# A gated cross-attention and mixture-of-experts layer: the opening by pairs of tiles with two sum-free products first, smaller key stores, and the last routing step's rows at the far end of each expert's slots

## The chip, the cores and the metric

The kernel runs on one core of one Trainium2 chip. The metric is the device time of one execution in microseconds (us), of which several runs are taken; one further execution is profiled.

## The reference, cut to what matters

All data is float32. x is 4096 rows of 512, ctx is 3202 rows of 512.

```python
def attn(hc, hq):            # hc = layernorm(x), hq = ctx
    Sim = (hc @ w1)[:, None] + (hq @ w2)[None, :] + (hc * w3) @ hq.T + b_sim
    hq_hat = softmax(Sim, axis=1) @ hq
    hc_bar = softmax(Sim.max(axis=1)) @ hc
    feats  = concat([hc, hq_hat, hc * hq_hat, hc * hc_bar])
    return feats @ W_qv + b_qv

def moe(xf):                 # xf = layernorm(x), E = 8 experts, top 2, cap = 640 slots each
    gates = softmax(xf @ w_router + b_router)
    topv, topi = top_k(gates, 2)
    pos  = running count of earlier choices of the same expert
    keep = pos < cap
    buf[e, pos] = xf[token] where kept
    out  = gelu(buf @ w1 + b1) @ w2 + b2      # 512 -> 2048 -> 512 per expert
    y    = sum over the two choices of gate * out, divided by the sum of the kept gates
    return y

x = x + tanh(g_xattn) * attn(layernorm(x), ctx)
x = x + tanh(g_ffn)   * moe(layernorm(x))
```

Which slot of its expert a kept token gets does not matter, as long as no two tokens share one and the token is found again.

## The kernel before, in words

Nearly all matrix products are done as seven block products instead of eight (the Winograd form of Strassen's scheme): with a left matrix in blocks A11 to A22 and a right one in blocks B11 to B22, sums S1, S2, S4 (and A11 − A21) of the left and T1, T2, T4 (and B22 − B12) of the right are made on VectorE first. The products are named "1" (A11·B11), "2" (A12·B21), "6", "7", "5", "4", "3"; only "1" and "2" use raw blocks of both sides. Results are put together from the products by additions (u2, u3) on VectorE as they come.

The attention works on eight groups of 512 rows of x (a group is four tiles of 128 rows). For each group, stage S multiplies the scaled queries `Qp` with the key tiles: 12 tiles `kt` of 2 × 128 context rows in six pairs, one call of `chain` for each pair (product at L512), followed by 128 left-over rows. In group 0 (`stage_a_first`, `build`) the key tiles come raw from `ctxt_t`, a transposed copy of the context made on the host. VectorE adds the four sums (L364 to L368), and ScalarE's queue stores the whole tile of seven blocks to `kt_d`; later groups load these seven blocks with one transfer (`load_keys`). The stages D, E and V, with softmax and values, follow; they are not touched.

The opening comes before the first pair: `stage_a_first` loads four tiles of x on SyncE, and `layernorm` makes each one's statistics (L93, L95), its factor on GpSimd (L99, L100) and its normalised form (L102). TensorE transposes it (L110), ScalarE copies it to `qT`, and pieces `Qp` are made of two tiles at a time (L212, L214). `right_sums` makes the T blocks.

Each engine's instructions stand in one order, and an instruction that waits holds up all behind it on its engine. `tc.issue_after(i)` keeps an instruction behind another in that order. DMAs are issued from an engine's queue in the same order; SyncE's carries nearly all loads. SBUF tiles come from pools: `st` has five buffers for key tiles, so a sixth tile's load waits until the first one's tile has been read by TensorE and stored.

After the eight groups come the routing steps, in which 32 tiles are taken in steps of 4 (six times) and 2 (four times). For each step TensorE makes `x1p` (L1062), `choose` finds the two experts of each row on VectorE, and `place` counts the slots (`pos`, L1167 and L1168) and writes the slot numbers `sidx`. `dispatch` scatters each tile's rows to `buf_d` in DRAM with one indirect DMA per choice (L1198, on GpSimd's queue; 64 in all). The steps are overlapped: a step's rows are placed and sent while the next is computed. Behind the last step there is nothing to overlap with; `idle_work` gives TensorE 7 and then 11 matmuls of no use (`idle`, L1218).

The experts come last. `expert_in` loads five tiles `xb` of 128 rows from an expert's 640 slots (L1335), transposes them (L110) and makes the T blocks. For each half of the hidden layer there are four calls of `seven` (f = 0 to 3, 28 products of 128×320, L1299), with Gelu on ScalarE (L1421), then the output products (`op`, L1462). For expert 0 each of the five loads is made to wait for every scatter:

```python
if e == 0:
    for i in scatters:
        tc.add_manual_dep(ld.ins, i.name, ..., reason="every token is in its slot")
```

The scatters are declared free of dependences among themselves, because their slots are distinct.

Of the kernel before, what the change touches and what calls it, by code (L numbers as in the profile page):

```python
# [20 lines left out]
def gated_layer(ctx, tc, x, x_t, ctxt, ctxt_t, ctxt_c, ctxt_r, g_xattn, g_ffn, w_sim, w_sim_r, b_sim, W_qv, W_qv_t, b_qv, b_qv_c, w_router, b_router, w1, b1, w2, b2, out):  # L21
# [35 lines left out]
    nc.scalar.dma_start(ws, w_sim)  # L57
# [4 lines left out]
    nc.scalar.dma_start(bsim, b_sim.partition_broadcast(P))  # L62
    gx = const.tile([P, 1], F32, name="gx")
    nc.scalar.dma_start(gx, g_xattn.partition_broadcast(P))
    gf = const.tile([P, 1], F32, name="gf")
    nc.scalar.dma_start(gf, g_ffn.partition_broadcast(P))
    bqv = const.tile([P, D], F32, name="bqv")
    tgx, tgf = gx, gf
    nc.scalar.activation(tgx, gx, AF.Tanh)
    nc.scalar.activation(tgf, gf, AF.Tanh)  # L70
# [13 lines left out]
    nc.scalar.dma_start(wrc, w_router.rearrange("(c p) e -> p c e", p=P))  # L84
    we = const.tile([P, 4, DC, E], F32, name="we")
    sd = const.tile([P, NT], F32, name="sd")

    scales, normed = [], []

    def layernorm(sm, dst, src, t):  # L90
        st = sm.tile([P, 6], F32, name=f"st{t}", tag="st")
        with tc.issue_after(normed[-2]) if len(normed) > 1 else ExitStack():
            nc.vector.bn_stats(st, src)  # L93
        mv = sm.tile([P, 2], F32, name=f"mv{t}", tag="mv")
        nc.vector.bn_aggr(mv, st)  # L95
        rstd = sm.tile([P, 1], F32, name=f"rstd{t}", tag="rstd")
        ve = sm.tile([P, 1], F32, name=f"ve{t}", tag="ve")
        with tc.issue_after(scales[-1]) if scales else ExitStack():
            nc.gpsimd.tensor_scalar(ve, mv[:, 1:2], EPS, None, ALU.add)  # L99
        scales.append(nc.gpsimd.tensor_tensor(rstd, ve, neghalf, ALU.pow).ins)  # L100
        nc.gpsimd.tensor_tensor(sd[:, t : t + 1], ve, rstd, ALU.mult)
        nrm = nc.vector.tensor_scalar(dst, src, mv[:, 0:1], rstd, ALU.subtract, ALU.mult)  # L102
        normed.append(nrm.ins)
        return nrm

    def transposed(pool, src, name):

        ps = pool.tile([P, DC, P], F32, name=name, tag="tr")
        for c in range(DC):
            nc.tensor.transpose(ps[:, c, :], src[:, c * P : (c + 1) * P], ident)  # L110
        return ps

# [11 lines left out]
    with ExitStack() as s1:  # L124
# [10 lines left out]
        kt_d = [dram.tile([P, 7, 2, P], F32, name=f"kt_d{j}", tag=f"kt_d{j}") for j in range(NJ)]  # L135

        kc_d = dram.tile([P, 4, 2, P], F32, name="kc_d", tag="kc_d")
        KSLOT = {"1": 0, "2": 1, "7": 2, "4": 3, "5": 4, "6": 5, "3": 6}
# [8 lines left out]
        nc.scalar.dma_start(bcol, b_qv_c)  # L147
# [17 lines left out]
        nc.scalar.dma_start(cr, ctxt_r)  # L165
# [19 lines left out]
        def right_sums(g, qT, Qp):  # L185

            B11, B12, B21, B22 = (Qp[:, r : r + 2, c : c + 256] for r in (0, 2) for c in (0, 256))
            T1, T2, T4 = (sb.tile([P, 2, 256], F32, name=f"q{k}_{g}", tag=f"qt{k}") for k in (1, 2, 4))
            tt(T1, B12, B11, ALU.subtract)
            t2 = tt(T2, B22, T1, ALU.subtract)  # L190
            tt(B12, B22, B12, ALU.subtract)
            tt(T4, B21, T2, ALU.subtract)
            live[g] = {"qT": qT, "t2": t2, "B": {"1": B11, "6": T2, "7": B12, "5": T1, "2": B21, "4": T4, "3": B22}}

        def stage_a_first():

            qT = sb.tile([P, DC, TG], F32, name="qT0", tag="qT", bufs=2)
            Qp = sb.tile([P, DC, TG], F32, name="Qp0", tag="Qp")
            qs = []
            for t in range(4):  # L200
                q = sb.tile([P, D], F32, name=f"q{t}", tag="q" if t < 3 else "mb", bufs=3 if t < 3 else 1)
                nc.sync.dma_start(q, x[t * P : (t + 1) * P, :])
                layernorm(sm, q, q, t)
                ps = transposed(ps_tr, q, f"qps{t}")
                cp = nc.scalar.copy(qT[:, :, t * P : (t + 1) * P], ps)
                qs.append(q)
                if t % 2:
                    h = slice((t - 1) * P, (t + 1) * P)
                    for c in range(DC):
                        w3, w2 = ws[:, 2 * DC + c : 2 * DC + c + 1], ws[:, DC + c : DC + c + 1]  # L210
                        if c < DC // 2:
                            qp = ts(Qp[:, c, h], qT[:, c, h], w3, w2, ALU.mult, ALU.add)  # L212
                        else:
                            live["qp"] = nc.scalar.activation(Qp[:, c, h], qT[:, c, h], AF.Identity, scale=w3, bias=w2)  # L214
                    if t == 1:
                        live["norm"] = qp
                if t == 2:
                    with tc.issue_after(cp.ins):
                        nc.scalar.dma_start(wv[:, 0, :], w_sim_r[:D].partition_broadcast(P))
                        nc.scalar.dma_start(  # L220
                            wv[:, 1:, :].rearrange("p r d -> p (r d)"), ctxt[L - NR :, :].flatten().partition_broadcast(P)
                        )
                        nc.scalar.dma_start(bqv, b_qv.partition_broadcast(P))
            right_sums(0, qT, Qp)
            nc.scalar.dma_start(qT_d[0], qT)
            return qs
# [10 lines left out]
        def stage_a_rest(qs):  # L237
# [13 lines left out]
            ps = ps_tr.tile([P, DC, P], F32, name="wrps", tag="tr")[:, 0, :E]  # L251
            for c in range(DC):
                nc.tensor.matmul(ps, ones, wrc[:, c, :], start=c == 0, stop=c == DC - 1)
            mean = be
            ts(mean, ps, 1.0 / D, None, ALU.mult)
            tt(wrc, wrc, mean.unsqueeze(1).to_broadcast([P, DC, E]), ALU.subtract)
# [100 lines left out]

        def build(j):

            kt = st.tile([P, 7, 2, P], F32, name=f"ktb{j}", tag="st")  # L360
            queue.append(nc.sync.dma_start(kt[:, 0:4].rearrange("p a b w -> p (a b) w"), ctxt_t[:, j, :, :]))
            A11, A12, A21, A22, S1, S2, S4 = (kt[:, k, :, :] for k in range(7))
            with tc.issue_after(live["norm"].ins if j < 2 else live[0]["t2"].ins):
                tt(S1, A21, A22, ALU.add)  # L364
                tt(S2, S1, A11, ALU.subtract)
            with tc.issue_after(live[0]["t2"].ins):
                tt(S4, A12, S2, ALU.subtract)
                tt(A21, A11, A21, ALU.subtract)  # L368
            return kt
# [60 lines left out]
        def load_keys(g, j):  # L430
            kt = st.tile([P, 7, 2, P], F32, name=f"kt{g}_{j}", tag="st")
            queue.append(nc.sync.dma_start(kt, kt_d[j]))
# [26 lines left out]
        def chain(name, prod, done):  # L459
# [5 lines left out]
            prod(pa, "1", True, False)  # L465
# [6 lines left out]
            tt(u2, p6, p1, ALU.add)  # L472
# [7 lines left out]
            prod(pa, "2", False, True)  # L480
            nc.scalar.copy(done(0, 0), pa)  # L481
# [6 lines left out]
        def stage_s(g):  # L488
# [4 lines left out]
            kts = {}  # L493
            if g == 0:
                for j in PAIRS[0]:
                    kts[j] = build(j)
            for jj, js in enumerate(PAIRS):
                if g == 0:
                    for j in PAIRS[jj + 1] if jj + 1 < len(PAIRS) else []:
                        kts[j] = build(j)  # L500
# [16 lines left out]
                e_add = chain(f"s{g}_{jj}", prod, lambda i, j: e[:, j, i, :, :])  # L517
                if g == 0:
                    for j in js:
                        nc.scalar.dma_start(kt_d[j], kts[j])  # L520
# [454 lines left out]
    with ExitStack() as s2:  # L975
# [49 lines left out]
        scatters = []  # L1025


        STEPS = [list(range(t, t + G)) for t in range(0, NT - 2 * G, G)]
        STEPS += [list(range(t, t + G // 2)) for t in range(NT - 2 * G, NT, G // 2)]
# [18 lines left out]
        def tile_mm(s, i):  # L1048
# [11 lines left out]
            for j in range(2):  # L1060
# [5 lines left out]
            stt(  # L1066
                x1.rearrange("p (j d) -> p j d", j=2), ps[:, :, :256], tgx, r[:, :, :256], ALU.mult, ALU.add,
                accum_out=s.sum[:, i : i + 1],
            )
# [23 lines left out]
        def choose(s):  # L1093
# [56 lines left out]
            for i in range(n):  # L1150
# [6 lines left out]
                tt(dst, s.base[:, i, :], s.mask[:, i, :], ALU.add)  # L1157

        def place(s):
# [16 lines left out]
            ts(keep, keep, float((E + 1) * CAP), None, ALU.is_lt)  # L1176

# [16 lines left out]
            if s.next is not None and s.next.n == 2:  # L1194
                placed.append(done.ins)

        def dispatch(s, i, k):
# [8 lines left out]
            scatters.append(sc.ins)  # L1206

            tc.declare_no_dep(scatters[-1], group="scatters", reason="slots are unique")
            tc.add_to_no_dep_group("scatters", scatters[-1])
# [3 lines left out]
        placed = []  # L1213
        def idle_work(mm, n):

            for _ in range(n):
                with tc.issue_after(mm.ins):
                    mm = nc.tensor.matmul(idle, ones, wv[:, 0, :], start=True, stop=True)  # L1218
# [3 lines left out]
        prev, s = None, begin(0)  # L1222
# [3 lines left out]
        def send(n):  # L1226
            for _ in range(min(n, len(routed))):
                dispatch(*routed.pop(0))
# [6 lines left out]
        for g in range(len(STEPS)):  # L1235
# [5 lines left out]
            if s.n > 2:  # L1241
                with tc.issue_after(mm.ins):
                    place_prev()
                send(4)
                for i in range(2, s.n):
                    tile_mm(s, i)
            sc = scale(s)
            if s.n == 2:
                with tc.issue_after(mm.ins):
                    place_prev()  # L1250
            with tc.issue_after(sc.ins):
                send(4 if s.n > 2 else 5)
# [4 lines left out]
        idle_work(prev.counted, 11)  # L1257
# [8 lines left out]
    with ExitStack() as s3:  # L1266
# [28 lines left out]
        def seven(tag, n, A11, A12, A22, S1, S2, S3, S4, B11, B21, B22, T1, T2, T3, T4, done):  # L1295

            def prod(ps, A, B, start=True, stop=True):
                for i, (a, b) in enumerate(zip(A, B)):
                    nc.tensor.matmul(  # L1299
# [254 lines left out]
```

## Time and profile before

| | us |
|---|---|
| median of 4 runs | 2638.25 (2637.54 to 2639.9) |
| profiled execution, its own time | 2638.75 |
| its span, first to last instruction | 2636.7 |
| TensorE busy | 2606.5 |
| VectorE busy | 1703.2 |
| ScalarE busy | 461.5 |
| GpSimd busy | 237.3 |
| first attention product starts | 12.91 |
| routing steps end, hand-over begins | about 1607 |
| first product of expert 0 starts | 1631.67 |
| output products of expert 0 start | 1664.01 |

Starts are counted from the first instruction. A matmul line of the profile groups several records; a product of stage S is eight records (two tiles × two blocks, two records for each matmul), and a product of an expert is four. The mean granted clock of TensorE over the span is 0.995.

### The profile page before, as it was taken

How to read it: one execution, taken by the hardware profiler on the slowest of the kernel's cores; microseconds unless marked ns; L12 is line 12 of the kernel's file. 1: busy time of each engine (PE TensorE's matmuls, PEld its weight loads, DVE VectorE, ACT ScalarE, POOL GpSimd, SP SyncE). 2: the span in 40 equal slices, each digit the busy share in tenths (PEclk: the TensorE clock that was granted, in tenths of full speed). 3: DMA queues.
4: the chain of work that ended last, by engine and by line, in shares of the span. 5: the costliest groups of instructions: out<-in, count | busy, mean ns of one | idle time of the engine just before them, and what ended most of it. 6: DMA issues, size and time to landing. Idle time of an engine off the chain costs nothing. (4 is left out here: it accounts for less than half of the span.)

```text
span 2636.7 us, 29718 instructions
## 1 busy us (share of the span) xinstructions
PE 2606.5 (99%) x11236; PEld 2103.1 (80%) x11236; DVE 1703.2 (65%) x3412; ACT 461.5 (18%) x796; POOL 237.3 (9%) x288
## 2 busy tenths in 40 slices
PE   8999999999999999999999999999999999999998
PEld 7748888888888888888888886777777777777776
DVE  7858856947668569478475567464756565565654
ACT  1201201201102002012020143112121111111111
POOL 0111000000001000000000055010101010101010
PEclk9999999999999999999999999999999999999999
DMA  8497656746746657467446795131324132322210
GB/s 314 152 284 243 212 175 190 246 147 180 255 159 195 220 160 241 161 186 248 154 140 207 265 356 185 65 124 64 128 78 144 67 128 89 104 92 100 76 60 21
DMA packets 182959, 436.07 MB, mean 165 GB/s; under 512 B 17454, under 2 KB 84270, under 8 KB 180768
## 3 DMA queue, kind: packets, MB, share of 16 engines
q1 hardware_dynamic: 150208, 352.25, 40.6%
q0 software_dynamic: 16096, 45.04, 5.0%
q10 hardware_dynamic: 16512, 36.88, 3.9%
q8 instruction: 89, 1.46, 0.2%
q14 instruction: 54, 0.44, 0.1%
HBM read 355.71 MB, written 85.55 MB: 167 GB/s over the span
## 5 line engine op out<-in xcount | busy, mean ns | idle before, releaser
L512 PE MATMUL pas<-Qp,kt 128*128 128x256 f32 x672 | 160.5, 380 | 0.0
L1299 PE MATMUL pah<-bT,w 128*128 128x320 f32 x512 | 159.8, 434 | 0.5 <-ACT p1h L1306 0.5
L662 PE MATMUL pbv<-E,vt 128*128 128x256 f32 x672 | 147.3, 379 | 0.0
L662 PEld LDWEIGHTS pbv<-E,vt 128*128 128x128 f32 x672 | 127.7, 190 | 17.3
L512 PEld LDWEIGHTS pas<-Qp,kt 128*128 128x128 f32 x672 | 127.2, 190 | 17.4 <-issue 0.5
L1299 PEld LDWEIGHTS pah<-bT,w 128*128 128x128 f32 x512 | 97.3, 190 | 39.7 <-ACT p1h L1306 1.0
L603 ACT ACTIVATE E<-E 128x1024 f32<-128x1024 f32 x96 | 100.9, 1057 | 129.5 <-DVE E L602 128.7
L602 DVE TENSOR_TENSOR E<-E,mb 128x1024 f32<-128x1024 f32 x96 | 116.0, 1224 | 11.4 <-ACT mb L589 11.4
L1299 PE MATMUL pao<-w,h 128*128 128x256 f32 x512 | 120.9, 379 | 0.0
L1485 POOL DMA_INDIRECT out<-acc,ti x40 | 41.0, 1024 | 852.8 <-DVE acc L1484 843.1
L1062 PE MATMUL x1p<-W,q2T 128*128 128x264 f32 x512 | 116.1, 387 | 0.0
L1462 PE MATMUL op<-w,h 128*128 128x512 f32 x256 | 114.8, 593 | 0.0
L1299 PEld LDWEIGHTS pao<-w,h 128*128 128x128 f32 x512 | 97.3, 190 | 20.0 <-issue 7.7
L1062 PEld LDWEIGHTS x1p<-W,q2T 128*128 128x128 f32 x512 | 96.7, 190 | 16.1
L468 ACT COPY p1s<-pas 128x512 f32<-128x512 f32 x48 | 28.2, 586 | 437.4 <-issue 257.1
L538 DVE TENSOR_TENSOR M<-M,E 128x1024 f32<-128x1024 f32 x80 | 98.0, 1225 | 4.3
L693 PE MATMUL vv<-E,vc 128*128 128x512 f32 x192 | 94.3, 622 | 0.5 <-ACT E L603 0.5
L1462 PEld LDWEIGHTS op<-w,h 128*128 128x128 f32 x256 | 46.6, 190 | 48.7 <-issue 43.0
L1423 DVE TENSOR_TENSOR h<-p4h,u3h 128x320 f32<-128x320 f32 x64 | 31.3, 490 | 78.0 <-PE p4h L1299 78.0
L481 ACT COPY E<-pas 128x512 f32<-128x512 f32 x48 | 28.1, 585 | 303.8 <-PE pas L512 286.7
L611 DVE TENSOR_TENSOR SM<-SM,E 128x1024 f32<-128x1024 f32 x64 | 78.6, 1227 | 2.5 <-ACT E L603 2.5
L484 DVE TENSOR_TENSOR E<-p4s,u3s 128x512 f32<-128x512 f32 x48 | 33.1, 689 | 72.2 <-PE p4s L512 72.2
(449 smaller groups left out, 5467.8 us busy)
## 6 DMA issues: line engine op xcount, KB each, us to landing
kt<-kt_d SPq DMA_DIRECT2D x84, 896.0 KB, 4.7
w<-in_w SPq DMA_DIRECT2D x32, 2048.0 KB, 9.2
vt<-vs_d SPq DMA_DIRECT2D x56, 768.0 KB, 7.1
wp<-wt_d SPq DMA_DIRECT2D x56, 520.0 KB, 4.6
kt_d<-ktb ACTq DMA_DIRECT2D x12, 896.0 KB, 4.6
buf_d<-zero SPq DMA_DIRECT2D x80, 129.0 KB, 5.9
xb<-buf_d SPq DMA_DIRECT2D x40, 258.0 KB, 4.0
r<-r_d SPq DMA_DIRECT2D x32, 260.0 KB, 6.2
```

Of the source, the lines that this page charges most:

```text
L484: tt(done(1, 0), p4, u3, ALU.add)
L512: nc.tensor.matmul(ps[:, jl, :], kts[j][:, KSLOT[p], k, :], B[p][:, k, :], start=start and jl == 0 and k == 0, stop=stop and k == 1, skip_ ...
L538: tt(M, M, e[:, :, h], ALU.max)
L602: live[g]["last"] = tt(e, e, m, ALU.subtract)
L603: live[g]["exp"] = nc.scalar.activation(e, e, AF.Exp)
L611: tt(SM, E_t[0][:, lr] if jj == 1 else SM, E_t[jj][:, lr], ALU.add)
L662: nc.tensor.matmul(ps[b], vt[:, j - i * JH, b * P : (b + 1) * P], right(j) if j < NJ else right_c, start=start and j == 0 and b == 0, stop ...
L693: mm = nc.tensor.matmul(ps[b], vc[:, h, b * P : (b + 1) * P], E[j // 2][:, :, h, j % 2, :] if j < NJ else ec, start=j == 0 and h == 0, sto ...
L1062: mm = nc.tensor.matmul(ps[:, j, :B1], qTs[g][:, c, q * P : (q + 1) * P], W1[:, c, j, :], start=(c == 0), stop=(c == DC - 1))
L1299: nc.tensor.matmul(ps, a, b, start=start and i == 0, stop=stop and i == len(A) - 1, skip_group_check=True)
L1462: nc.tensor.matmul(ps, hT[:, k, 2 * MH :], W2[:, k, :], start=(k == 0), stop=(k == KH - 1))
L1485: sc = nc.gpsimd.indirect_dma_start(out=out[:, :], out_offset=rows_of(ti, s), in_=acc[:, :], in_offset=None, bounds_check=N - 1, oob_is_er ...
```

## The change

Four things are changed.

1. *Opening.* The constants' loads are issued on ScalarE after a Tanh of one column that needs no load, and five matmuls of no use (`warm`) and the router-mean matmuls come first on TensorE. The four x loads are issued back to back, then the raw key tiles of pair 0. Statistics and factors are made for two tiles at a time, then the four normalisations, in a written-out order. The context's transposed copy has its second half rolled so that the raw blocks come as A11, A12, A22, A21. In the first pair `chain` runs the products "1" and "2" first, into separate banks, and adds their results on VectorE; the key sums are interleaved with the query pieces and the right sums.
2. *Key tiles.* `kt_d` holds only the four sums (512 KB for a tile instead of 896 KB); later groups load each tile with two transfers, the raw blocks from `ctxt_t` and the sums from `kt_d`. The stores of group 0 are issued behind the pair's copy of result (0, 0).
3. *Routing steps.* Their sizes are 4 (five times), 3, 3, 2, 2, 2. The last step's rows are numbered down from the end of each expert's slots instead of on from the rows before: one matmul more (`first`, total count per expert before the step) and four small VectorE operations. There are 5 instead of 11 idle matmuls behind the last count, and their moving operand is `ident`.
4. *Hand-over.* Of expert 0's five row loads the first three are given manual dependences on all scatters but the last step's four (`late`), the other two on all. After the transposes of tiles 0 to 2 TensorE runs the products A11·B11 and A12·B21 of all four f (the last pair after the other two tiles' transposes), and `seven` leaves these out.

The diff, cut:

```diff
+        kt_d = [dram.tile([P, 4, 2, P], F32, name=f"kt_d{j}", tag=f"kt_d{j}") for j in range(NJ)]
-        KSLOT = {"1": 0, "2": 1, "7": 2, "4": 3, "5": 4, "6": 5, "3": 6}
+        KSLOT = {"1": 0, "2": 1, "4": 2, "7": 3, "5": 4, "6": 5, "3": 6}
...
         def stage_a_first():
+            with tc.issue_after(nc.scalar.activation(junk, ones[:, 0:1], AF.Tanh).ins):
+                constants()
+            warm = bank("warm").rearrange("p a b -> p (a b)")
+            for _ in range(5):
+                mm = nc.tensor.matmul(warm, ones, ones.unsqueeze(1).to_broadcast([P, 4, P]), start=True, stop=True)
+            wr = bank("wrps")[:, 0, :E]
+            for c in range(DC):
+                with tc.issue_after(mm.ins):
+                    mm = nc.tensor.matmul(wr, ones, wrc[:, c, :], start=c == 0, stop=c == DC - 1)
...
+            keys = [load_raw(j) for j in PAIRS[0]]
...
+            for h in (0, 2):
+                st_ = [sm.tile([P, 6], F32, name=f"st{t}", tag="st") for t in (h, h + 1)]
...
+            S = [key_sums(kt) for kt in keys]
+            last = in_turn(last, [lambda c=c: queries(0, c) for c in range(DC)] + S[0][:2])
+            last = in_turn(last, [lambda c=c: queries(1, c) for c in range(DC // 2)])
+            with tc.issue_after(last.ins):
+                live["sums"] = right_sums(0, qT, Qp, S[1][:2])
+            live["sums"] = in_turn(live["sums"], S[0][3:] + S[1][3:] + S[0][2:3] + S[1][2:3])
...
         def load_keys(g, j):
-            queue.append(nc.sync.dma_start(kt, kt_d[j]))
+            nc.sync.dma_start(kt[:, :3].rearrange("p a b w -> p (a b) w"), ctxt_t[:, j, :6, :])
+            queue.append(nc.sync.dma_start(kt[:, 3:], kt_d[j]))
...
-        def chain(name, prod, done):
+        def chain(name, prod, done, first=False):
             pa = bank(f"pa{name}")
-            prod(pa, "1", True, False)
+            prod(pa, "1", True, first)
+            if first:
+                p2 = bank(f"p2{name}")
+                prod(p2, "2", True, True)
...
+            if first:
+                tt(done(0, 0), p2, p1, ALU.add)
+            else:
+                prod(pa, "2", False, True)
+                live["copied"] = nc.scalar.copy(done(0, 0), pa)
...
                     for j in js:
-                        nc.scalar.dma_start(kt_d[j], kts[j])
+                        with tc.issue_after(live.get("copied", live["qp"]).ins):
+                            nc.scalar.dma_start(kt_d[j], kts[j][:, 3:])
...
-        STEPS = [list(range(t, t + G)) for t in range(0, NT - 2 * G, G)]
-        STEPS += [list(range(t, t + G // 2)) for t in range(NT - 2 * G, NT, G // 2)]
+        STEPS, sizes = [], [G] * (NT // G - 3) + [3, 3, 2, 2, 2]
...
         def choose(s):
...
+            if s.next is None:
+                before = T("before", [P, 2, n, E])
+                tt(before, s.first.unsqueeze(1).unsqueeze(1).to_broadcast([P, 2, n, E]), s.oh, ALU.mult)
+                s.far = T("far", [P, 2, n])
+                red(s.far, before, AX.X, ALU.add)
+                stt(s.far, s.rv, -float(CAP), s.far, ALU.mult, ALU.add)
...
         def place(s):
...
+            if s.next is None:
+                stt(pos, s.far, float((E + 1) * CAP - 1), pos, ALU.add, ALU.subtract)
...
-            scatters.append(sc.ins)
-            tc.declare_no_dep(scatters[-1], group="scatters", reason="slots are unique")
-            tc.add_to_no_dep_group("scatters", scatters[-1])
+            (scatters if s.next is not None else late).append(sc.ins)
+            tc.declare_no_dep(sc.ins, group="scatters", reason="slots are unique")
+            tc.add_to_no_dep_group("scatters", sc.ins)
...
         for g in range(len(STEPS)):
...
+            if s.next is None:
+                s.first = ps_mm.tile([P, 2, 512], F32, name="first", tag="mm")[:, 0, :E]
+                with tc.issue_after(mm.ins):
+                    mm = nc.tensor.matmul(s.first, ones, s.base[:, 0, :], start=True, stop=True)
...
-        idle_work(prev.counted, 11)
+        idle_work(prev.counted, 5)
...
-        def expert_in(e):
+        def expert_in(e, amid=None):
...
                 if e == 0:
-                    for i in scatters:
+                    for i in scatters if (s + 1) * P <= CAP - len(late) // 2 * P else scatters + late:
                         tc.add_manual_dep(...)
-                ps = transposed(ps_tr, xb, f"bps{e}_{s}")
+                with tc.issue_after(behind.ins) if behind is not None else ExitStack():
+                    ps = transposed(ps_tr, xb, f"bps{e}_{s}")
...
+                if amid is not None and s * P < HC <= (s + 1) * P:
+                    between = amid(*([xT[:, k, :HC] for k in c] for c in ((0, 1), (2, 3))))
+                    behind = [next(between) for _ in range(KQ - 1)][-1]
+            if amid is not None:
+                between.send(moved[-1])
...
+        def early_products(B11, B21):
+            early["h"] = hT = cb.tile([P, KH, CAP], F32, name="h0_0", tag="h")
+            mm = None
+            for f in range(KQ):
+                A11, A12 = ([a[:, k, f * P : (f + 1) * P] for k in range(2)] for a in w1s[:2])
+                pa = bank(f"pe{f}")[:, :HC]
+                with tc.issue_after(mm.ins) if mm is not None else ExitStack():
+                    prod(pa, A11, B11, stop=False)
+                early[f] = cb.tile([P, D], F32, name=f"e1_{f}", tag=f"o{f}")[:, :HC]
+                nc.scalar.copy(early[f], pa)
+                last = prod(pa, A12, B21, start=False)
+                nc.scalar.activation(hT[:, f, :HC], pa, AF.Gelu, bias=b1_t[:, f : f + 1])
+                mm = yield last
```

## The prediction

> **What bounds the kernel now.** I read the page first (spans, busy times), then the waits of TensorE, then the timeline of the two places where those waits lie, last the granted clock there. Page, first part:
>
> ```profile
> span 2636.7 us, 29718 instructions
> PE 2606.5 (99%) x11236; PEld 2103.1 (80%) x11236; DVE 1703.2 (65%) x3412; ACT 461.5 (18%) x796; POOL 237.3 (9%) x288
> ```
>
> TensorE sets the time: 2636.7 − 2606.5 = 30.2 us is all it ever idles. A change that removes no matmuls can win only that, and what runs slow for its clock. TensorE's waits say where most of it lies (columns: tile and line, releaser, total, times, longest):
>
> ```profile
> PE qps L110 <- DVE q L102: 8.7, 3, 6.3
> PE bps L110 <- DMA xb<-buf_d: 4.3, 2, 3.7
> PE pbs L512 <- DVE E L479: 2.4, 2, 2.2
> PE pos L1167 <- DVE mask L1149: 1.5, 6, 0.6
> ```
>
> The first is the opening (layernorm of four x tiles), the second the hand-over from routing to expert 0, the third a stall in the second pair of key tiles. After the last matmul 8.6 us of tail follow, which the change doesn't touch. Opening, in the timeline (start, duration, engine, line, operation):
>
> ```profile
> 6.32 1.12 PE L110 MATMUL qps<-ident,q 128*128 128x128 f32 x4 [6.32 <-DVE q L102]
> 12.91 2.93 PE L512 MATMUL pas<-Qp,ktb 128*128 128x256 f32 x8
> 26.93 1.89 PE L512 MATMUL pas<-Qp,ktb 128*128 128x256 f32 x8
> 34.23 0.43 DVE L364 TENSOR_TENSOR ktb<-ktb 128x256 f32<-128x256 f32 x1 [5.07 <-DMA ktb<-in_ctxt_t]
> 39.62 1.99 PE L512 MATMUL pbs<-Qp,ktb 128*128 128x256 f32 x8 [2.17 <-DVE E L479]
> ```
>
> The same eight records cost 2.93 us at 12.91 and 1.89 at 26.93: TensorE starts slow. The clock column reads 1.00 in both windows, so I go by the durations. Products start 1.73 us apart when warm, so a pair of key tiles (seven) is 12.1 us; pair 0 takes 26.93 − 12.91 = 14.0. The stall at 39.62 begins on VectorE, which waited 5.07 us for a key tile whose buffer was still being stored.
>
> Hand-over:
>
> ```profile
> 1613.99 9.69 PE L1218 MATMUL idle<-wv,ones 128*128 128x512 f32 x22
> 1622.29 0.97 POOL L1198 DMA_INDIRECT buf_d<-xn,sidx  x1 [0.30 <-issue]
> 1624.66 2.22 SPq L1335 DMA_DIRECT2D xb<-buf_d  x5
> 1627.42 1.94 PE L110 MATMUL bps<-ident,xb 128*128 128x128 f32 x8 [3.74 <-DMA xb<-buf_d]
> 1634.57 1.34 PE L1299 MATMUL pah<-bT,w 128*128 128x320 f32 x4 [0.52 <-ACT p1h L1306]
> 1635.91 1.34 PE L1299 MATMUL p6h<-x,w1s 128*128 128x320 f32 x4
> ```
>
> The last scatter starts at 1622.29, the row loads follow, and at 1635.91 `p6` of f = 0 starts with 2 of the half's 28 products done. Granted clock by window (before the DMA share, column PEclk):
>
> ```profile
> 1626.00:1627.40 1.40, 0.00 (x0) 0.01 (x1) 0.00 (x0) 0.00 (x0) 0.00 (x0) 0.53 1.10 313
> 1627.40:1632.00 4.60, 4.03 (x17) 3.32 (x18) 0.80 (x2) 1.17 (x2) 0.00 (x0) 0.50 0.99 358
> 1632.00:1633.00 1.00, 1.00 (x3) 0.50 (x3) 0.59 (x1) 0.00 (x0) 0.00 (x0) 0.54 1.05 418
> 1633.00:1640.00 7.00, 6.49 (x26) 4.19 (x25) 5.79 (x27) 2.78 (x4) 1.44 (x2) 1.00 1.03 391
> ```
>
> After the 3.74 us gap everything runs at half clock until about 1633.
>
> **Opening, start.** Today tile 3 is normalised last, at 11.34, because its statistics wait for its load (8.42). Its load was issued at 3.70 behind the other three; the changed order issues four back to back at the 0.33 us that an issue takes. I put its landing at 6.0, from the second tile's statistics at 4.92 plus two issues and slack. Two statistics of 0.69 and two of 0.18, a batched power of 0.6 on GpSimd, and four normalisations of 0.55 give 7.5 to 9.5 for the latter. Four transposes of a tile (1.12) and a copy (0.59) end at 11.5; the first four `Qp` pieces (0.37 each on VectorE) let product "1" start at 10.95. I allow up to 12.0, since eight pieces and four key sums now stand in one VectorE order. Today it is 12.91. Five filler matmuls (0.88 each by the 9.69 us of eleven, twice that at half clock) run from about 1.1 to between 5.5 and 10, ahead of the transposes. If they leave the clock up, the first product costs 1.89, not 2.93: −1.04. The router-mean matmuls (0.95 at 15.7) move out of pair 0. Against it, product "7" needs the last two key sums behind the right sums and I count 0.8 of new stall. Working through it: "1" 10.95, "2" 12.7, "6" 14.5, "7" 17.0, the rest 1.73 each, end 23.9 against 26.93: **−3.0**, bounds −1.3 (start at 12.0, half clock kept for a product) and −3.8 (no stall).
>
> **Opening, pair 1.** Key stores shrink from 7 slots (896 KB) to 4 (512 KB), twelve of them, but each is now issued behind the pair's ScalarE copy, so up to 9 us later. Pair 0 has no such copy, and its two stores go out by the end of the queries; the sixth tile's buffer comes free earlier and the load that landed at 34.2 has 384 KB less ahead of it per store (at 400 GB/s, the window's rate, 1 us each). The stall of 2.17 should go: **−2.0**. Bounds 0 and −2.2. Later pairs: VectorE is about 70% busy from 27 to 54 and a late tile 7 (I expect it at 43 to 44, with 2 us to spare) would hand the time back; that is the reason for the bound at 0.
>
> **Key tiles of groups 1 to 7.** The three raw blocks now come from the context (384 KB) and the four sums from the store (512 KB): 84 extra issues on SyncE, 0.33 to 0.44 us each, same bytes. The rows of before show `kt<-kt_d` landing in 4.7 us, and TensorE has no wait on a key tile after group 0. Each buffer is released some 12 us ahead of use, so about 6 us cover the added half microsecond: **0**, bounds 0 and +3; if that cover were gone, each of 84 tiles would pay its 0.4 us, some 34 us in all.
>
> **Routing steps.** The tiles run 4×5, 3, 3, 2, 2, 2 instead of 4×6, 2×4: the same 256 matmuls and one step fewer at the position wait (1.5 us over six). The held-back `x1` of a second tile costs VectorE nothing it isn't waiting for. **0**, bounds ±0.5.
>
> **Hand-over.** Here the change claims most. The last step's rows go to the far end of each expert's slots, so that tiles 0 to 2 of expert 0 could be loaded before the last four scatters; eight early products then fill TensorE. But I looked up which semaphore counts the first row load waits for in the built program: one is the count that only the last of the late scatters reaches (224 on its lane; the scatters of the step before give 208). The five loads stand in order on SyncE, so all still wait for the last scatter. So the far-end part buys nothing, and its costs stay. Its three VectorE operations in the choice (0.2 each) overlap the position matmul in part, one more stands in the placement chain, and the `first` matmul ahead of it costs 0.3; the chain of 1613.2 to 1616.2 grows by about 0.5, the loads go out at 1625.1. Six idle matmuls fewer lengthen TensorE's gap from 3.74 to about 9 us, which is idle either way. Then, by the row durations: transposes of tiles 0 to 2 from 1627.9 at half clock, third copy on ScalarE to 1632.1. The early products run from there with two stalls (1.05 behind the 1.28 us Gelu table load and the first Gelu, 0.65 for the last f), transposes of tiles 3 and 4 between them. `p6` of f = 0 starts at 1644.2 with 8 done, so 20 × 1.076 = 21.5 remain: 1665.7. Today 26 remain at 1635.91: 1664.0 (the trace starts the output products at 1664.01). **+1.8**, bounds 0 (stalls hidden) and +4 (VectorE, which needs 22.2 us for what then lies beside 21.5 of TensorE, becomes late).
>
> The row for the clock is the half-clock stretch of 1626 to 1633: it ended 5.5 us after the first transpose and 1.3 us after the first product, so it can't tell which of the two counted. The Trainium skill, "TensorE: Matmul & The Clock Gate", Part 1 (The HAM clock gate), says an idle window of about 3.4 us halves the clock and as much busy time restores it, and Part 4 (PE-mode transpose) that transposes don't count as busy. By that rule the longer gap and the early products at 1632.1 would run half speed to 1635.5 and my +1.8 would be about +3; by the row alone, which recovered sooner, it stays +1.8.
>
> **Sum.** −3.0 − 2.0 + 0 + 0 + 1.8 = −3.2 on the profiled execution of 2638.75 (span 2636.7 and 2.05 around it): 2635.5. That execution lies 0.5 over the median of the runs, 2638.25, so I forecast 2635.0. A measurement of this kernel can tell ±0.2% (5.3 us) from no change: faster means under 2633.0, slower over 2643.5.
>
> **Rivals.**
> *The far end works.* If the first three loads do wait only for the step before's scatters (ending about 1617.3), they go out at 1619.2, early products start at 1622.4 and `p6` at 1634.7 with 8 done: 1634.7 + 21.5 = 1656.2, −7.8 in place of +1.8, total 2625.4. For: the manual dependencies in the code say so. Against: the count in the program. A mistake in my reading is what it needs: 0.15.
> *The opening gains nothing.* Loads run at 400 GB/s in the window of 13 to 27 and VectorE is 12 of 14 us busy there; the products begin earlier and wait for sums and tiles instead. With −1.3, 0 and +1.8: about 2638.8. 0.24.
> *Slower: key tiles late.* Split loads queue on SyncE behind other in-order waits; the six pairs of seven groups then stall. It decides from the point where a tile lands over 6 us later than today (4.7 us landing today); at 0.2 us a tile over that, 84 tiles are +17, total 2652. For: one load became two and both must land. Against: SyncE issues cost 0.4 and no wait on `kt` exists now. 0.12.
> *Forecast*: 0.49, own range 2631 to 2639.
>
> **Numbers.** Faster: 0.15 from the far end, and 0.19 from the forecast's lower end (opening −6.0 and hand-over 0 give 2632.2) and from gains in the routing steps: 0.34. Slower: 0.12 plus 0.01 from the no-gain rival with hand-over +4: 0.13. Same: 0.53. The range 2625.0 to 2641.5 takes in the centres of the first two rivals; the slower one and half of the far end's case, about 0.19, lie outside.
>
> **What would show it.** Right: product "1" before 11.5 with records of 0.22; no `pbs` wait in pair 1; row loads of expert 0 after the last scatter; a TensorE gap near 9 us and half clock behind it; output products of expert 0 about 3.2 us earlier than at 1664.0. Wrong: row loads starting before the late scatters; any TensorE wait on `kt` in groups 1 to 7; a stall in pairs 2 to 4 equal to what pairs 0 and 1 won.

## The result and the profile after

The changed kernel takes 2641.98 us (median of 37 runs, 2638.42 to 2650.63) against 2638.31 of the kernel before (57 runs): ratio 1.0014, 95% interval 1.0009 to 1.0018. It is slower by 3.7 us, where a gain of 3.2 was forecast, and 0.5 us outside the range. That is less than the 5.3 us which the prediction took for the smallest change that can be told, but with so many runs the interval lies clear of 1. The profiled execution took 2640.82 us. Line numbers in what follows are those of each run's own kernel: L110 of the kernel before is L85 in the changed one, L512 is L565, L1167 is L1237. The first part of the page, and the longest waits of TensorE (tile and line, releaser, total, times, longest):

```profile
span 2639.0 us, 29839 instructions
PE 2607.7 (99%) x11236; PEld 2103.1 (80%) x11236; DVE 1702.7 (65%) x3418; ACT 461.3 (17%) x795; POOL 227.7 (9%) x281
```

```profile
PE bps L85 <- DMA xb<-buf_d: 9.2, 1, 9.2
PE pos L1237 <- DVE mask L1212: 4.4, 7, 3.1
PE pad L917 <- issue: 2.3, 1, 2.3
PE qps L85 <- DVE q L234: 1.5, 2, 1.0
```

The waits of the opening went from 8.7 to 1.5 and the stall of 2.2 in pair 1 is gone; the wait for the rows grew from 3.7 to 9.2, as foreseen. The new line is the second: one wait of 3.1 us at the position matmul of a routing step. Four starts from the timelines tell where the span of 2636.7 became 2639.0:

| start of | before | after | difference | made in this stretch |
|---|---|---|---|---|
| first product of group 1 | 200.44 | 196.22 | −4.2 | opening −4.2 |
| first `x1p` of the routing | 1483.82 | 1478.66 | −5.2 | groups −0.9 |
| first idle matmul | 1607.36 | 1607.33 | 0.0 | routing +5.1 |
| last product | 2627.97 | 2630.28 | +2.3 | hand-over +2.3 |

The opening and the hand-over did about what was forecast (−5.0 and +1.8). The routing steps, put at 0 ± 0.5, lost more than the opening had won. The place, in the timeline of after (GpSimd, VectorE and TensorE lines, others left out):

```profile
1567.20 0.97 POOL L1270 DMA_INDIRECT buf_d<-xn,sidx  x1 [3.82 <-issue]
...
1571.03 0.97 POOL L1270 DMA_INDIRECT buf_d<-xn,sidx  x1 [0.30 <-issue]
1572.07 0.19 POOL L1153 TENSOR_SCALAR rstd<-ssd 128x3 f32<-128x3 f32 x1
...
1573.27 0.18 DVE L1168 TENSOR_TENSOR lg<-lg,rstd 128x24 f32<-128x24 f32 x1 [4.97 <-POOL rstd L1154]
...
1577.32 0.37 PE L1237 MATMUL pos<-mask,upper 128*128 128x24 f32 x2 [3.10 <-DVE mask L1212]
```

`rstd`, the factor that `choose` begins with, needs the sums of squares `ssd` of the step's last tile. ScalarE had them at 1568.8:

```profile
1568.62 0.19 ACT L1135 ACTIVATION_READ_ACCUMULATOR jx<-x,sum 128x1 f32 x1
```

GpSimd made `rstd` only at 1572.07, behind four scatters of the step before, queued one each 1.27 us. VectorE waited 4.97 us for it and TensorE 3.10 for VectorE. In a step of four the same four scatters stand ahead of the factor, but its `ssd` comes one tile (3.6 us) later. The last step of four in the kernel before:

```profile
1572.24 0.97 POOL L1198 DMA_INDIRECT buf_d<-xn,sidx  x1 [3.83 <-issue]
...
1576.07 0.97 POOL L1198 DMA_INDIRECT buf_d<-xn,sidx  x1 [0.30 <-issue]
1577.50 0.19 POOL L1090 TENSOR_SCALAR rstd<-ssd 128x4 f32<-128x4 f32 x1 [0.46 <-ACT jx L1072]
```

The scatters had ended at 1577.0, and the factor waited for ScalarE. A step of three with that many scatters ahead has no such room. The gap costs a second time (granted clock in the column behind POOL):

```profile
1574.20:1577.60 3.40, 0.30 (x3) 0.30 (x2) 3.07 (x18) 2.75 (x8) 2.48 (x4) 1.00 0.49 109
1577.65:1581.06 3.41, 3.41 (x10) 2.79 (x10) 2.93 (x16) 1.01 (x3) 0.70 (x1) 0.50 0.91 272
```

After 3.4 us with 0.30 of work TensorE ran 3.41 us at half clock, which is 1.7 more: 3.1 + 1.7 = 4.8 of the 5.1. And the hand-over:

```profile
1624.76 2.22 SPq L1423 DMA_DIRECT2D xb<-buf_d  x5
...
1627.49 2.92 PE L85 MATMUL bps<-ident,xb 128*128 128x128 f32 x12 [9.16 <-DMA xb<-buf_d]
...
1644.63 1.24 PE L1380 MATMUL p6h<-x,w1s 128*128 128x320 f32 x4
```

All five loads still go out after the last scatter (1622.38, 0.97), at 1624.76 (1625.1 was forecast), and `p6` starts at 1644.63 (1644.2).

### The profile page after: what moved, and what is told of

Its sections match the earlier page's. It is cut to its first block, busy times and chain, and to the rows that moved or that the text cites. A ratio compares the mean times of both kernels' runs of the same rounds, so it can differ in the third digit from the quotient of the medians.

```text
span 2639.0 us, 29839 instructions
## 1 busy us (share of the span) xinstructions
PE 2607.7 (99%) x11236; PEld 2103.1 (80%) x11236; DVE 1702.7 (65%) x3418; ACT 461.3 (17%) x795; POOL 227.7 (9%) x281
## 5 line engine op out<-in xcount | busy, mean ns | idle before, releaser
L565 PE MATMUL pas<-Qp,kt 128*128 128x256 f32 x672 | 160.5, 380 | 0.0
L1380 PE MATMUL pah<-bT,w 128*128 128x320 f32 x480 | 148.8, 432 | 0.0
L565 PEld LDWEIGHTS pas<-Qp,kt 128*128 128x128 f32 x672 | 127.1, 190 | 17.4 <-issue 0.5
L661 ACT ACTIVATE E<-E 128x1024 f32<-128x1024 f32 x96 | 101.4, 1058 | 129.9 <-DVE E L660 128.7
L1380 PEld LDWEIGHTS pah<-bT,w 128*128 128x128 f32 x480 | 91.2, 190 | 36.4
L1380 PE MATMUL p7h<-bT,w 128*128 128x320 f32 x256 | 79.5, 432 | 0.0
L565 PE MATMUL pbs<-Qp,kt 128*128 128x256 f32 x336 | 79.5, 379 | 0.0
L1380 PE MATMUL pbh<-bT,w1s 128*128 128x320 f32 x256 | 79.5, 433 | 0.0
```

Of the source, the lines that this page charges most:

```text
L565: nc.tensor.matmul(ps[:, jl, :], kts[j][:, KSLOT[p], k, :], B[p][:, k, :], start=start and jl == 0 and k == 0, stop=stop and k == 1, skip_ ...
L661: live[g]["exp"] = nc.scalar.activation(e, e, AF.Exp)
L1380: mm = nc.tensor.matmul(ps, a, b, start=start and i == 0, stop=stop and i == len(A) - 1, skip_group_check=True)
```

## The experiments

All are edits of the changed kernel, but for one of the kernel before. Ratios are to the kernel before on the same chip, with 95% intervals.

**The step sizes.** `e1_steps`:

```diff
-        STEPS, sizes = [], [G] * (NT // G - 3) + [3, 3, 2, 2, 2]
+        STEPS, sizes = [], [G] * (NT // G - 2) + [2, 2, 2, 2]
```

> The changed kernel with the step sizes of before (six of 4, four of 2), all else as changed. Theory (the steps of three cost 5.0 us: a 3.10 us gap of TensorE before the position matmul at 1577 and a half-clock window of 3.41 us behind it): both vanish, the span falls from 2639.0 to 2634 (2633 to 2635), 2 to 3.5 us under before. Rival (the loss lies in the hand-over or in the held-back x1 and the sends in order, and the steps only showed it): it stays at 2637.5 to 2639.5, over before.

Measured: 2636.1 us, ratio 0.999 (0.9981 to 0.9999), span 2634.2. From the first `x1p` to the first idle matmul 123.5 us, as before (123.5), against 128.7 after. The largest wait at a position matmul is 0.29. The changed kernel also holds some of the routing's instructions behind others that the list of the change doesn't name (`scaled` and `chosen` in the code); this run keeps them. So the step sizes carry the loss.

**GpSimd's order.** `e2_send` keeps the steps of three:

```diff
-                    send(4)
+                    send(4 if s.n > 3 else 1)
...
-                send({4: 4, 3: 3, 2: 5}[s.n])
+                send({4: 4, 3: 6, 2: 5}[s.n])
```

> The changed kernel with its steps of 3, but in those steps one scatter instead of four is queued on GpSimd ahead of the step's factor, and six instead of three behind it. Theory (GpSimd's order: rstd stood ready at about 1568.8 and ran at 1572.1 behind four scatters of 1.27 us): the gap at 1577 falls from 3.10 to under 0.5, the half-clock window goes, span 2634 (2633 to 2635.5). Rival (VectorE's chain of choose is too long for a step of three, whatever GpSimd does): the gap stays over 2 us and the span over 2637.

Measured: 2636.86 us, ratio 0.9989 (0.9981 to 0.9998), span 2632.4; routing 124.0. Its timeline at the same place, to be read against the one above:

```profile
1567.39 0.97 POOL L1270 DMA_INDIRECT buf_d<-xn,sidx  x1 [3.82 <-issue]
1569.10 0.19 POOL L1153 TENSOR_SCALAR rstd<-ssd 128x3 f32<-128x3 f32 x1 [0.73 <-ACT jx L1135]
...
1570.29 0.18 DVE L1168 TENSOR_TENSOR lg<-lg,rstd 128x24 f32<-128x24 f32 x1 [1.80 <-POOL rstd L1154]
...
1574.46 0.37 PE L1237 MATMUL pos<-mask,upper 128*128 128x24 f32 x2
```

The factor now waits for ScalarE's squares and not for the queue, it runs 3.0 us earlier, and the position matmul has no wait of its own. Three scatters moved behind one operation settle the rival: VectorE's chain fits well into a step of three. The clock stays at 1.00 there.

**The wait that held the loads.** `e3_loads`:

```diff
+                    if (s + 1) * P <= CAP - len(late) // 2 * P:
+                        for i in late:
+                            tc.declare_no_dep(ld.ins, i.name, reason="the late rows lie behind these")
```

> The changed kernel, but the first three row loads of expert 0 are also freed of the automatic wait on the last step's scatters, whose rows lie behind theirs. Theory (that one wait count holds all five loads back): the loads go out at 1618 to 1620 instead of 1624.8, TensorE's 9.2 us gap falls to 3 to 4, and the output products start 7 to 10 us earlier than 1666; span 2629 to 2632. Rival (the loads were not what was late: ScalarE's copies and Gelus and VectorE's sums take the gain): loads earlier, but the output products gain under 3 us; span over 2636.

Measured: 2631.42 us, ratio 0.9974 (0.9966 to 0.9983), span 2630.0, with the routing loss still in it (129.1). From the first idle matmul to the last product it takes 1012.7 us; before 1020.6, after 1022.9. The gap:

```profile
1621.16 0.63 PE L85 MATMUL bps<-ident,xb 128*128 128x128 f32 x4 [1.62 <-DMA xb<-buf_d]
```

The loads start at 1618.36, while the last step's scatters still run (1618.53 to 1624.6). So the automatic dependence of these loads on the late scatters undid what the manual dependences were written for, and the part of the change that was to bring most brought nothing because of it.

**Opening and key tiles alone.** `e4_opening`: step sizes, numbering, hand-over and eleven idle matmuls as before.

> Opening and key tiles as changed; step sizes, numbering, idle matmuls and hand-over as before (without the early products). Theory (opening and key tiles bring 4.2 us by the second group and nothing takes them back): span 2631 to 2633, 4 to 6 us under before. Rival (split key loads cost something later, or routing gives it back): 2635.5 or more, within 1.2 us of before.

Measured: 2634.25 us, ratio 0.9987 (0.9978 to 0.9996), span 2631.0. The second group starts at 194.97 (−5.5), and from there to the routing it takes 1284.0 us (before 1283.4): the 84 added loads cost nothing that these profiles show, and TensorE waits for no `kt` in any profile.

**Stores of seven blocks.** `e5_fullstore` is `e4_opening` with

```diff
-            nc.sync.dma_start(kt[:, :3].rearrange(...), ctxt_t[:, j, :6, :])
-            queue.append(nc.sync.dma_start(kt[:, 3:], kt_d[j]))
+            queue.append(nc.sync.dma_start(kt, kt_d[j]))
...
-                            nc.scalar.dma_start(kt_d[j], kts[j][:, 3:])
+                            nc.scalar.dma_start(kt_d[j], kts[j])
```

> The opening alone (as e4_opening) with the key stores and loads of before: seven blocks stored for each tile, one load of 896 KB in later groups. Theory of the prediction (the stall in pair 1 went because the stores shrank by 384 KB): a stall of 1 to 2.2 us comes back in pair 1 or 2, the first product of the second group at 196 to 197.2 instead of 195.0. Rival (it went because the loads and sums were ordered anew): 194.5 to 195.5, same time as e4_opening; then the split loads cost and bring nothing either way.

Measured: 2637.37 us, ratio 0.9993 (0.9984 to 1.0002), second group at 198.77, 3.8 later than in `e4_opening`. The waits of TensorE from 20 to 110 us have two lines that `e4_opening` does not have:

```profile
PE pas L564 <- DMA ktb<-in_ctxt_t: 1.1, 2, 0.6
PE pbs L564 <- DVE E L531: 1.0, 1, 1.0
```

They lie at 73 to 80 us, in the last pairs; the third pair's `p6` still starts at 38.49 (38.24 in `e4_opening`, 43.18 before). The product that starts at 76.17 in `e4_opening` starts at 79.64 here, so 3.5 of the 3.8 are lost by then, 2.1 of them in these two waits. So both theories fall in part. The stall in pair 1 went by the new order, not by the smaller stores. This order is not of loads and sums alone: in the kernel before five stores have been issued by 25.2 us, here the third follows only at 33.57. Before, then this run:

```profile
18.15 2.67 ACTq L520 DMA_DIRECT2D kt_d<-ktb  x3
23.74 1.47 ACTq L520 DMA_DIRECT2D kt_d<-ktb  x2
```

```profile
18.31 0.85 ACTq L577 DMA_DIRECT2D kt_d<-ktb  x2
33.57 0.81 ACTq L577 DMA_DIRECT2D kt_d<-ktb  x2
```

Which part of the order did it is not shown. With the stores going out later, full-size ones make the last key tiles late; the smaller stores pay for that. A longer half-clock stretch at 98.5 us (6.83 instead of 3.41) adds at most the other 0.3, since `e4_opening` waited 1.3 us for ScalarE at that place. This rests on one profile of each run; the intervals of the two ratios overlap.

**Fillers.** `e8_nowarm` is `e4_opening` with one filler matmul instead of five.

> The opening alone (as e4_opening) with one filler matmul instead of five. Theory (the five fillers bring the clock up before the first product, where they are not followed by a pause of a whole window): the first products run at half clock for 2 to 4 us, the first product of the second group 1 to 1.8 us later than 195.0. Rival (the fillers are idle time that changes nothing): 194.5 to 195.5.

Measured: 2635.47 us, ratio 0.9994 (0.9984 to 1.0003), second group at 198.17. The third pair's `p6` is 1.34 us later than in `e4_opening` (39.58 to 38.24); 1.9 more follow from 94.5 us on, where a half-clock stretch is 10.24 instead of 3.41. In the first 14 us the cost lies mostly in the transposes ahead of the products: sixteen records take 3.76 us here (0.235 each), eight take 1.08 in `e4_opening` (0.135 each). The column of the granted clock reads 1.00 there all the same. The intervals of the two ratios overlap, so what the fillers bring is read from one profile each.

**The gap and the clock.** `e7_idle16` is the kernel before with 16 instead of 11 idle matmuls.

> The kernel before with 16 instead of 11 idle matmuls behind the last count, which fills the gap ahead of the row loads. Theory (the gap of 3.74 us is what halves the clock): no half-clock window at the hand-over, transposes of 0.27 instead of 0.45, output products 1.5 to 3 us earlier than 1664.0. Rival (transposes don't hold the clock up, as the Trainium skill, 'TensorE: Matmul & The Clock Gate', Part 4, says): a half-clock window comes behind the transposes all the same and the gain is under 1 us.

Measured: 2636.34 us, ratio 0.9989 (0.9981 to 0.9998); idle matmul to last product 1019.1 instead of 1020.6. The clock there (third column from the end):

```profile
1627.38:1630.79 3.41, 2.42 (x17) 1.71 (x16) 1.38 (x2) 1.31 (x3) 0.00 (x0) 1.00 1.02 370
1630.79:1634.20 3.41, 2.90 (x11) 1.75 (x11) 3.02 (x4) 1.45 (x3) 0.00 (x0) 1.00 1.02 401
```

The first of these windows holds row transposes, a pause of 0.88 and only in its last 0.5 us products; full clock followed. The rival, a half-clock window behind the transposes, did not come. The output products start 1.5 us earlier by their distance from the idle matmuls (55.1 us instead of 56.65). That is the lower end of what the theory gave: half clock costs only what work lies in it, 4.93 us in before.

**Both mends.** `e6_all` is the edits of `e2_send` and `e3_loads` together.

> Both mends together in the changed kernel: one scatter ahead of the factor in steps of 3, and the first three row loads freed of the last step's scatters. Theory (the two losses are independent, 4.6 us by routing and 10 by the hand-over against the changed kernel): span 2624 to 2627, about 11 us under before. Rival (with routing earlier the scatters of the step before are later than TensorE's idle work and the loads wait for them instead): the gap ahead of the transposes grows from 1.6 to over 4 us and the span stays over 2628.

Measured: 2626.96 us, ratio 0.996 (0.9947 to 0.9972), span 2625.0, the lowest ratio of all. The load gap is 2.46 us, so the rival's wait is there, but small. Routing 124.0, idle matmul to last product 1014.2.

**Without early products.** `e10_noearly` is `e6_all` with `nxt = expert_in(0)`.

> e6_all without the eight early products: expert 0's first three tiles still come early, TensorE goes on with the usual order. Theory (the gain of the freed loads is TensorE's work between the transposes; without it the first sums wait for the last row load, 7 us later): a TensorE gap of 4 to 7 us behind the third tile's transposes, span 2631 to 2634. Rival (early loads alone are worth it): within 2 us of 2625.

Measured: 2637.65 us, ratio 0.9989 (0.998 to 0.9998), span 2639.3. TensorE transposes three tiles and then waits:

```profile
1633.22 1.94 PE L85 MATMUL bps<-ident,xb 128*128 128x128 f32 x8 [7.30 <-DMA xb<-buf_d]
```

The gap is there, a little over the 4 to 7 us of the theory; the span is well over it, because 5.4 us of it lie in the routing (129.4 instead of 124.0, see the next experiment). Idle matmul to last product is 1020.1, about as with the old hand-over (1019.9 in `e4_opening`), but that stretch begins with seven idle matmuls that half clock made 2.7 us longer here. From the last count, behind these seven, to the last product it takes 1011.3 us, against 1013.6 in `e4_opening` and 1008.1 in `e6_all`. So the early loads alone are worth about 2.3 us at the hand-over, and the eight products that stand in the room they make another 3.2.

**Filling the pauses.** `e9_fill` is `e6_all`, `e11_four_two` has the step sizes of before in its place, and `e12_four_two_fill` is that with the fillers:

```diff
-        idle_work(prev.counted, 5)
+        idle_work(prev.counted, 7)
...
-            for _ in range(5):
+            for _ in range(6):
```

> e6_all with seven instead of five idle matmuls behind the last count and six instead of five fillers at the start: TensorE's pauses of 2.46 us ahead of the row transposes and 1.11 us ahead of the first transposes are filled. Theory (pauses that take half of a 3.41 us clock window cost that much of half clock later): no half-clock window at 10.8 and none at 1615, span 1.5 to 3 us under e6_all's 2625.0. Rival (the windows fall by chance, and the fillers only delay the transposes): within 1 us of 2625, or over it.

> The changed kernel with the step sizes of before and the first three row loads freed. Theory (the steps of three bring nothing that the steps of four and two don't): span 2624.5 to 2627.5, as e6_all (2625.0), and no routing gap over 0.6 us. Rival (the sizes 3, 3, 2, 2, 2 send the scatters earlier and so free the loads earlier): 1.5 us or more over e6_all, with a longer gap ahead of the row transposes.

> The same with seven idle matmuls behind the last count and six fillers at the start (as e9_fill, whose routing steps met waits on VectorE that its rivals did not have). Theory (the pauses cost half clock): 1 to 2.5 us under e11_four_two, no half-clock window in the first 20 us or at the hand-over. Rival: within 0.7 us of it; the windows fall by their phase.

Measured: 2633.04 (0.9968, 0.9956 to 0.998), 2630.06 (0.9964, 0.9951 to 0.9977) and 2630.19 us (0.9962, 0.9949 to 0.9975). In `e9_fill` the half-clock windows at 10.8 and at the hand-over are gone, as expected, but idle matmul to last product is 1013.6 against 1014.2 in `e6_all`: the fillers bring 0.6 us at the hand-over at most, and `e12_four_two_fill` is no faster than `e11_four_two`, which has no half-clock window at either place without them. With the scatters in order, the step sizes make no difference that these runs can tell: the ratios of all three lie inside the interval of `e6_all`. In these three and in `e10_noearly`, though, the routing took 126.5 to 129.4 us, with waits at the position matmuls of up to 2.75 us that the same routing code did not have in `e1_steps`, `e2_send` and `e6_all`. VectorE waited there, at `x` (L1129), 1.4 to 4.5 us for something that the profile calls remote; the records of these traces do not say what it is. That stays open. The profile after has no such wait in its routing, so it is not needed for the changed kernel's own loss.

## Why the prediction was wrong

*Routing steps, "0, bounds ±0.5": the step that failed.* It counted matmuls (the same 256 products) and the number of position waits, and left out what stands in GpSimd's queue ahead of the factor. Measured +5.1, shown by `e1_steps` (undone: −5.1) and `e2_send` (the order alone: −4.6). All that was needed stood in the trace of before: the factor of a step of four ran 0.5 us behind the last of four scatters, so a step shorter by a tile of 3.6 us had to wait about 3.

*Opening, −3.0 − 2.0: near in sum, partly wrong in its parts.* Measured −4.2 in the profile after, and −3.6 to −5.5 in the seven other profiles that have the whole opening. The first pair brought 1.7 instead of 3.0 in the profile after: product "1" started at 11.94 and not at 10.95, the stall of 0.8 did not come, and the first product ran at half clock (granted clock 0.50 from 10.93 to 14.34, first product 3.08 us instead of 1.89). The window before that stretch held 1.87 us of work in 3.41; whether that is the cause is not shown, since in `e10_noearly` a window with 1.79 at the same place was not followed by half clock. Pair 1 brought 2.4 where 2.0 was forecast, but not by the smaller stores to which the prediction put it (`e5_fullstore`).

*Key tiles of groups 1 to 7, 0: right* (`e4_opening`). The slower rival, key tiles late, had the sign and not the place.

*Hand-over, +1.8: right.* Measured +2.3, with the loads held by the count that was named. The half clock lasted until 1635.68, 13.65 us in all, where the skill's rule had put its end at 1635.5; the +3 by that rule and the +1.8 by the row bracket what was measured. The rival "the far end works" was worth −7.8 in its reckoning; with the wait taken away it is −7.9 (`e3_loads`, whose hand-over has no half-clock stretch).

*The sum.* −4.2 − 0.9 + 5.1 + 2.3 = +2.3 in the two profiled spans; the medians differ by 3.7. The tail behind the last matmul is 8.4 us in both, where the prediction read 8.6. Of what the groups show, −0.9, the larger part is a half-clock stretch behind 1451 us that was 3.41 long instead of 6.83.

## What to carry to other kernels

When pieces of a pipelined loop are made smaller, look at every in-order queue that the loop shares: work of the piece before that used to end in time may now stand ahead of what the next piece needs first. A dependence that is written out by hand doesn't loosen one that is drawn automatically; count the waits of the built program before pricing what it should release, and price both outcomes. An earlier load is worth more when work stands ready to be put behind it: here 2.3 us without and 5.4 with.

## What the runs showed of the hardware that was not expected

Half clock comes in stretches of 3.41, 6.83, 10.24 and 13.65 us in these traces (but for the one in which each span ends), one to four of the same window. In the kernel before they start at 100.34, 1455.43 and 1626.10, which is 397 and 50 windows of 3.413 apart, so the windows run on beside the kernel (the other traces agree); they start at another point in each execution. So the same code can cost a different number of them: the opening has a stretch of 3.41 in the profile after and in `e6_all` and none in `e1_steps` to `e4_opening`, and the stretch near 98 us was 3.41 in `e4_opening`, 6.83 in `e5_fullstore`, 10.24 in `e8_nowarm`. The Trainium skill, "TensorE: Matmul & The Clock Gate", Part 1 (The HAM clock gate), speaks of a free-running window of about 3.4 us, which agrees.

The page speaks of an idle window as what halves the clock; here partly busy ones did. The share of recorded work does not decide it either. Windows with 1.87 us of work in 3.41 (the profile after, 7.52) and 0.30 (1574.20) were followed by half clock; windows with 1.73 (`e4_opening`, 1617.02), 1.79 (`e10_noearly`, 8.18) and 2.42 (`e7_idle16`) were not. And in every trace there is a half-clock stretch that begins between 93 and 101 us; in the kernel before the window ahead of it was nearly full (second number), 2.21 us of it matmuls with 8 columns (`we`):

```profile
96.93:100.34 3.41, 3.17 (x23) 2.60 (x23) 1.85 (x6) 0.58 (x1) 0.38 (x1) 1.00 0.61 231
100.34:103.75 3.41, 2.90 (x12) 2.29 (x12) 3.39 (x3) 2.05 (x2) 0.00 (x0) 0.50 0.00 0
```

What the gate goes by was not tested.

Part 4 of the same page (PE-mode transpose) says that full clock does not engage for transposes, which do not count as busy in the same way; its figures are of bf16. The runs here speak against it for 128×128 float32 transposes. In `e7_idle16` a window whose work was transposes but for its last 0.5 us was followed by full clock. In `e2_send` the row transposes (1622.88 to 1625.83) had a window to themselves, the first product followed at 1626.50, and the clock was back at 1626.20:

```profile
1622.80:1626.20 3.40, 2.95 (x12) 2.27 (x12) 0.00 (x0) 1.51 (x3) 0.00 (x0) 0.50 1.01 342
1626.20:1629.60 3.40, 3.10 (x11) 1.98 (x12) 0.00 (x0) 0.68 (x2) 0.00 (x0) 1.00 1.02 398
```

`e6_all` shows the same: a half-clock window with 2.92 us of transposes alone, from 1615.09, then full clock at 1618.50, ahead of the first product at 1619.08. In the profile after, the half clock ended where the page's rule had put it (1635.68 for 1635.5): the window from 1628.85, with 2.75 us of transposes and products together, did not end it, and the next one, full of products, did. That row by itself agrees with the page; `e2_send` and `e6_all` do not.
